# Attention mixing of a spectral attention layer: rounds made ahead, transposes spread, loads moved forward, image products moved to the end

## The chip, the cores and the metric

The kernel runs on one core of one Trainium2 chip. The metric is device time in microseconds of one execution of the whole program, the median over three runs; lower is better.

The core has a tensor engine (PE in the profile; its weight loads are listed as PEld), a vector engine (DVE), a scalar engine (ACT), a general engine (POOL) and an engine that issues most transfers (SP; its queue is SPq). Each runs its own instructions in order, and they meet through semaphores. Transfers between the chip's DRAM and the on-chip memory (SBUF) are carried by 16 DMA engines. Matmuls write to PSUM, a small memory of eight banks, from which DVE and ACT read.

## What is computed

Two layers run one after the other, each added to its input. The first is a state-space layer with a scan and takes most of the time; it is not touched. The second is an attention layer on spectra. Cut to what matters, with B*T = 4*48 images of 48 x 128 and 32 heads:

```python
k = _fno_layer(xa_n, wK, wKs, bKs, (H // 2, W // 2))
q = _fno_layer(xa_n, wQ, wQs, bQs, (H // 2, W // 2))
v = _fno_layer(xa_n, wV, wVs, bVs, (H, W))
qs, ks, vs = (to_seq(q), to_seq(k), to_seq(v))       # B, 32 heads, T, h*w
scores = jnp.einsum('bhtd,bhsd->bhts', qs, ks) / np.sqrt(ks.shape[-1])
attn_w = jax.nn.softmax(scores, axis=-1)
out = jnp.einsum('bhts,bhsd->bhtd', attn_w, vs)
projd = _fno_layer(out, wP, wPs, bPs, (H, W))
attention = _inorm(projd + xa, norm_g[1], norm_b[1])
an = _inorm(attention, norm_g[2], norm_b[2])
m = _fno_layer(an, wM0, ...)                          # two more spectral layers, with norms and a gelu
m = _fno_layer(m, wM1, ...)
output = _inorm(m, norm_g[5], norm_b[5]) + attention
```

`_fno_layer` is a product of low frequencies with complex weights, plus a product of the images with one number per head. Since V, the attention and P are linear in the spectra, the kernel never makes V: it forms for each head the product of the weights of V and P (`dgt`), multiplies the spectra `dxt` by it, and mixes over heads and source images with the attention weights.

## The kernel before

**Queues and planner.** The program is written with tiles; the framework makes the semaphores and the addresses. An instruction emitted through `nc.` is placed by a planner: each engine takes, in the planner's own simulated time, the earliest instruction of the program that is ready there, so a later one may run ahead of one that waits. What is emitted through `on.` keeps the program's order. A tile with a tag has `bufs` buffers; a new one waits until the last reader of the tile that had its buffer is done. Pools lie over each other like a stack: when a pool is closed, the next takes its space, and its tiles wait for the last readers of what lay there.

**Opening (about 3710 to 3886 us).** Images are loaded and normed, their spectra `a2` made, the weight products made (`products`), and for the scores `qs`, `ks` and `s0`. Constants lie in the pools `const` and `small`.

**Scores (L1447 to L1544), pairs of images.** For each of two pairs: twelve steps `jn`. In each, two products `f` of 128 x 1536 (L1490; on POOL for every third `jn`, on DVE otherwise; five buffers) and 16 matmul records into `sc`, four PSUM banks with one buffer (L1497); then eight small products `s0` by `d_qk` of 48 rows (16 records, L1508). Between them the generator `keys` makes `dxt`: for each of 4 images and 4 groups `k`, eight products of `a2` with `fh` (L1462; 48 rows; 256 records in all), ACT copies (L1469), a POOL sum (L1474) and a write to DRAM (L1475); the tile `xt` and its bank have one buffer each. Of its 32 parts 18 are drawn in the first pair and 14 in the second. Then the softmax of the pair, group by group `g`: maximum, difference, exponential (ACT), sum, reciprocal, product `sn`, three transposes `pat` (L1535) and an ACT copy to `attn_c` (L1538). The next pair's `sc` needs the banks that these read.

**Mixing (L1551 to L1660).** 24 steps (k, pair, q), four rounds g each: 96 rounds. `fetch` (L1594) loads the spectra `xrep` of the next step in two transfers of 576 KB, two buffers; `fetch_weights` (L1585) loads `grep`, 576 KB each, six buffers: four at the start, and for a later k two at (k-1, 1, 1) and two at (k-1, 1, 2). These calls are all made at one place, where a step begins, and SP keeps their order. A round:

```python
nc.scalar.copy(gp[:, :, 0:NC], r[:, 0:2])                       # L1624: grep to PSUM
nc.vector.tensor_mul(v, gp[...], x[:, :, 0:2])                  # L1626: 128 x 1536
nc.gpsimd.tensor_mul(v3, r[:, 2:3]..., x[:, :, 2])              # L1630: 128 x 768
nc.tensor.matmul(acc[c][64 * b : ...], attn_c[...], v or v3)    # L1634: c in 0..2, b in 0..1
```

The matmuls of a round are 12 records; `v`, `v3` and `gp` have two buffers. After each twelve rounds (a block: one k, one pair) comes a **turn**: ACT copies `acc[0]` to `s1`, DVE makes three combinations from `s1` and from `acc[1]`, `acc[2]` in PSUM (L1645 to L1647), eight transposes (records `pz`, four and four, L1652) and two ACT copies bring them to `z2`. `acc` has one buffer per c, so the next block's matmuls wait for these readers. At k = 1 each pair has 48 records `pa` of image products (`mix_of_images`, L1564), and ACT copies them to `a0_bd`.

**The rest (from L1667).** Inverse transforms along h (`pe_p`, with the constant `ih`) and along w (`iw2`), then the two further spectral layers. `iw2`, `fw64` and `ih` are loaded at L1675, L1677 and L2094.

Of the kernel before, what the change touches and what calls it, by code (L numbers as in the profile page):

```python
# [962 lines left out]
def layer1(ctx, tc, io, x1_dram, out):  # L963
# [15 lines left out]
    small = ctx.enter_context(tc.tile_pool(name="l1_small", bufs=2, side="right"))  # L979
# [21 lines left out]
    gmat = load("gmat1", [128, 128], io["c_group"])  # L1001
# [5 lines left out]
    mean_m = const.tile([128, 32], F32, name="mean_m")  # L1007
    nc.gpsimd.memset(mean_m, 1.0 / (H * W))
    over_h = const.tile([H, H], F32, name="over_h")
    nc.gpsimd.memset(over_h, 1.0 / H)  # L1010
    over_w = const.tile([128, T], F32, name="over_w")
    nc.gpsimd.memset(over_w, 1.0 / W)

    g_of = const.tile([128, 2, 128], F32, name="g_of")
# [128 lines left out]
    a0_bd = const.tile([96, 2, 96], F32, name="a0_bd")  # L1143
    zp = ctx.enter_context(tc.tile_pool(name="l1_z", bufs=1))
# [18 lines left out]
    dxt = dram.tile([B, 4, T, 3 * NC], F32, name="dxt")  # L1163
# [12 lines left out]
    s0 = pe.tile([T, B, T], F32, name="s0")  # L1176
# [38 lines left out]
    def products():  # L1215
# [5 lines left out]
        with ExitStack() as pw:  # L1221
# [19 lines left out]
            nc.scalar.copy(n_col, pn[:, 0:4].rearrange("p (s z) -> p s z", z=2))  # L1241

# [59 lines left out]
    with ExitStack() as ph:  # L1302
# [133 lines left out]
        for b in range(B):  # L1436
            bs = slice(b * T, (b + 1) * T)
            p = psum.tile([128, 512], F32, tag="mm", name=f"ps0_{b}")
            for j in range(4):
                for c in range(2):  # L1440
                    v = plain[:, j, c, bs]
                    nc.tensor.matmul(p[0:T, 0:T], v, v, start=(j == 0 and c == 0), stop=False)
            nc.tensor.matmul(p[0:T, 0:T], u32[:, bs], u32[:, bs], start=False, stop=True)
            nc.scalar.copy(s0[:, b], p[0:T, 0:T])


    with ExitStack() as ph:  # L1447
        p2 = ph.enter_context(tc.tile_pool(name="l1_p2", bufs=2))
        pf = ph.enter_context(tc.tile_pool(name="l1_pf", bufs=5))
        ps_1 = ph.enter_context(tc.tile_pool(name="l1_ps1", bufs=1, space=PSUM))  # L1450
        pst = ph.enter_context(tc.tile_pool(name="l1_pst", bufs=2, space=PSUM))
        psx = ph.enter_context(tc.tile_pool(name="l1_psx", bufs=1, space=PSUM))

        def keys():

            for b in range(B):
                for k in range(4):
                    xt = p2.tile([T, 3, NC], F32, tag="xt", name=f"xt{b}_{k}", bufs=1)
                    for e in range(2):
                        p = psx.tile([128, 512], F32, tag="xt", name=f"pxt{b}_{k}_{e}")  # L1460
                        for i in range(4):
                            nc.tensor.matmul(  # L1462
                                p[0:T, i * 96 : (i + 1) * 96],
                                a2[:, 8 * k + 4 * e + i, b * T : (b + 1) * T],
                                fh,
                                start=True,
                                stop=True,
                            )
                        nc.scalar.copy(  # L1469
                            xt[:, 0:2].rearrange("t c (k y) -> t k c y", y=48)[:, 4 * e : 4 * e + 4],  # L1470
                            p[0:T, 0:384].rearrange("t (k c y) -> t k c y", c=2, y=48),
                        )
                        yield
                    nc.gpsimd.tensor_add(xt[:, 2], xt[:, 0], xt[:, 1])  # L1474
                    nc.sync.dma_start(dxt[b, k], xt.rearrange("r c n -> r (c n)"))  # L1475

        beside = keys()
        gp = ps_1.tile([128, 3, 4, NH], F32, name="gp_qk")
        nc.scalar.copy(gp, g_qk)
        scale = 2.0 * math.sqrt((H // 2) * (W // 2))  # L1480
        for pair in range(2):
            sc = ps_1.tile([128, 4, 512], F32, tag="sc", name=f"sc{pair}")
            for jn in range(12):
                j, n = divmod(jn, 3)
                shape = [128, NH, T]
                on_pool = jn % 3 == 2
                f = []
                for b in range(2):
                    f.append(pf.tile(shape, F32, tag="f", name=f"f{pair}_{jn}_{b}"))
                    (nc.gpsimd if on_pool else nc.vector).tensor_mul(  # L1490
                        f[b],
                        (g_qk if on_pool else gp)[:, n, j, :, None].to_broadcast(shape),
                        ks[:, j, n, 2 * pair + b, None].to_broadcast(shape),
                    )
                for g in range(4):
                    for b in range(2):
                        nc.tensor.matmul(  # L1497
                            sc[64 * b : 64 * b + 64, g, 0 : 8 * T],
                            qs[:, j, n, 2 * pair + b],
                            f[b][:, 8 * g : 8 * g + 8],  # L1500
                            start=(jn == 0),
                            stop=False,
                        )
                for _ in range(2 - jn % 2 if pair == 0 else 1 + jn % 2):
                    next(beside, None)
            for g in range(4):
                for b in range(2):
                    nc.tensor.matmul(  # L1508
                        sc[64 * b : 64 * b + T, g, 0 : 8 * T],
                        s0[:, 2 * pair + b],  # L1510
                        d_qk[:, 8 * g : 8 * g + 8],
                        start=False,
                        stop=True,
                    )
            for g in range(4):
                t = f"{pair}_{g}"
                v = sc[:, g, 0 : 8 * T].rearrange("p (h s) -> p h s", s=T)
                shape = [128, 8, T]
                mx = p2.tile([128, 8], F32, tag="mx", name=f"mx{t}")
                nc.vector.tensor_reduce(mx, v, AX.X, ALU.max)  # L1520
                s = p2.tile(shape, F32, tag="s", name=f"s{t}")
                nc.vector.tensor_sub(s, v, mx[:, :, None].to_broadcast(shape))
                nc.scalar.activation(s, s, AF.Exp, scale=scale)
                sm = p2.tile([128, 8], F32, tag="sm", name=f"sm{t}")
                nc.vector.tensor_reduce(sm, s, AX.X, ALU.add)
                nc.vector.reciprocal(sm, sm)
                sn = p2.tile([128, 3, 16, 8], F32, tag="sn", name=f"sn{t}")
                nc.vector.tensor_mul(
                    sn.rearrange("t q r h -> t h q r"),
                    s.rearrange("t h (q r) -> t h q r", r=16),  # L1530
                    sm[:, :, None, None].to_broadcast([128, 8, 3, 16]),
                )
                p = pst.tile([128, 512], F32, tag="tr", name=f"pat{t}")
                for q in range(3):
                    nc.tensor.transpose(  # L1535
                        p[:, q * 128 : (q + 1) * 128], sn[:, q].rearrange("t r h -> t (r h)"), ident
                    )
# [3 lines left out]
                )  # L1541
        for _ in beside:
            pass
    early.close()  # L1544

# [669 lines left out]
```

## Time and profile before

The three runs took 4520.93, 4521.48 and 4522.82 us; the median is 4521.48.

| | us |
|---|---|
| median of three runs | 4521.48 |
| the profiled execution, its own time | 4536.64 |
| its span, first to last instruction | 4534.9 |
| scores: first f to last copy to `attn_c` | 3886.5 to 4006.8 |
| mixing: first to last `acc` record | 4019.4 to 4262.8 |
| first record of `pe_p` | 4269.8 |
| DMA issues of `xrep`: 48 of 576 KB | 4006.3 to 4247 |
| DMA issues of `grep`: 16 of 576 KB | 4007.6 to 4198 |

How to read it: times of the stages count from the first instruction of the profiled execution. A row of a timeline gives the start, the length, the engine, the line, the operation with the tile that it writes and those that it reads, how many instructions are merged in it, and in brackets how long the engine was idle before it and what ended that. A row of the windows gives a stretch, its length, each engine's busy time with its count of instructions, the clock granted to the tensor engine as a share of full speed, the busy share of the DMA engines and their GB/s. One fp32 matmul or transpose of the program appears as two records.

### The profile page before, as it was taken

To read this page: it belongs to the slowest core of one execution; us is meant where nothing else is said; L and a number is where in the kernel's file an instruction comes from. 1 tells how busy PE (TensorE), PEld (TensorE's weight loads), DVE (VectorE), ACT (ScalarE), POOL (GpSimd) and SP (SyncE) were. 2 spreads that over 40 slices of the span, in tenths; PEclk is the share of its full clock that TensorE was granted. 3 is DMA by queue.
4 is the path that set the end of the run, shared out by engine and by line. 5 is a ranking of instruction groups with operands and counts; after the bars stand their busy time and mean duration, and the time that the engine had idled before them with its cause. 6 is when DMAs were issued, how large, how long until landed. Compare 5 with 4: busy or idle time off the path is not lost.

```text
span 4534.9 us, 73722 instructions
## 1 busy us (share of the span) xinstructions
PE 3854.2 (85%) x26212; PEld 2993.0 (66%) x26212; DVE 3854.3 (85%) x2646; ACT 3439.2 (76%) x6964; POOL 3356.7 (74%) x3523
## 2 busy tenths in 40 slices
PE   6989987888899878888998788878877885979877
PEld 3777776777777767776777677767776762535444
DVE  3888999999899999998999999989999974657446
ACT  3888888988888889887888899879998862323344
POOL 2777788988787889887878898978888961356432
PEclk9989999999999899998999999999999997989877
DMA  2333333333333333333333333434333332155536
GB/s 63 93 94 103 91 100 100 111 96 110 97 106 94 96 102 111 98 110 94 107 93 96 103 107 100 115 94 111 104 105 105 100 111 62 25 128 138 133 101 160
DMA packets 327068, 461.05 MB, mean 102 GB/s; under 512 B 112788, under 2 KB 295636, under 8 KB 325996
## 3 DMA queue, kind: packets, MB, share of 16 engines
q1 hardware_dynamic: 311904, 433.20, 35.0%
q10 hardware_dynamic: 14796, 23.13, 1.5%
q8 instruction: 208, 3.41, 0.3%
q14 instruction: 160, 1.31, 0.1%
HBM read 400.99 MB, written 55.44 MB: 101 GB/s over the span
## 4 chain that ended last, share of the span: by engine, by line
PE 35%; ACT 22%; DVE 21%; issue 12%; POOL 5%; DMA 3%; SPq 1%; ACTq 0%; DVEq 0%; POOLq 0%
DVE h L55 13%; PE yp L55 8%; ACT scaled L55 6%; PE pc L55 5%; DVE db L55 4%; ACT da L55 4%; PE da L55 4%; ACT decay L55 4%; PE pd L55 2%; POOL hc L55 2%; PE acc L1634 2%; ACT dt L55 2%; ACT turned L55 2%; PE pg L55 2%; PE pb L55 2%
## 5 line engine op out<-in xcount | busy, mean ns | idle before, releaser
L55 POOL TENSOR_TENSOR hc<-h,cbc 128x960 f32<-128x960 f32 (+1 forms) x1280 | 2546.1, 1991 | 565.4 <-PE yp L55 194.1
L55 DVE TENSOR_TENSOR_SCAN h<-da,carry,db 128x962 f32<-128x962 f32 (+1 forms) x640 | 1355.9, 2119 | 115.7 <-ACT da L55 97.3
L55 DVE TENSOR_TENSOR_SCAN h<-decay,carry,da 128x962 f32<-128x962 f32 (+1 forms) x640 | 1362.5, 2129 | 6.5 <-PE da L55 6.2
L55 PE MATMUL yp<-ident,hc 128*128 128x128 f32 (+1 forms) x9728 | 1268.6, 283 | 52.9 <-POOL hc L55 49.3
L55 PEld LDWEIGHTS yp<-ident,hc 128*128 128x128 f32 (+1 forms) x9728 | 1140.6, 145 | 217.5 <-issue 109.3
L55 ACT ACTIVATE scaled<-turned,bt 128x256 f32<-128x256 f32 (+1 forms) x2432 | 1035.5, 497 | 27.5 <-ACT turned L55 23.6
L55 ACT ACTIVATE da<-dt,a_neg 128x480 f32<-128x480 f32 (+1 forms) x1280 | 826.1, 645 | 187.9 <-DVE h L55 165.0
L55 ACT ACTIVATE decay<-dt,a_neg 128x480 f32<-128x480 f32 (+1 forms) x1280 | 799.1, 674 | 28.2 <-DVE h L55 23.6
L55 PE MATMUL da<-ident,scaled 128*128 128x128 f32 (+1 forms) x4864 | 646.5, 276 | 194.1 <-DVE h L55 178.5
L55 DVE TENSOR_TENSOR db<-du,pb 128x960 f32<-128x960 f32 (+1 forms) x640 | 699.0, 1092 | 110.1 <-PE pb L55 100.1
L55 PEld LDWEIGHTS da<-ident,scaled 128*128 128x128 f32 (+1 forms) x4864 | 543.8, 145 | 243.0 <-ACT scaled L55 97.9
L55 PE MATMUL pb<-ident,bt 128*128 128x128 f32 (+1 forms) x2432 | 376.6, 276 | 38.4 <-DVE db L55 38.4
L55 PEld LDWEIGHTS pb<-ident,bt 128*128 128x128 f32 (+1 forms) x2432 | 292.7, 141 | 171.4 <-issue 98.2
L55 PE MATMUL pc<-pad,w_c 128*128 128x480 f32 (+1 forms) x720 | 335.9, 581 | 6.5 <-ACT th L55 3.0
L55 POOL TENSOR_TENSOR du<-dt,xc 128x480 f32<-128x480 f32 (+1 forms) x160 | 206.4, 1290 | 49.5 <-ACT dt L55 49.5
L1630 POOL TENSOR_TENSOR v<-grep,xrep 128x768 f32<-128x768 f32 x96 | 174.8, 1823 | 89.8 <-PE acc L1634 47.5
L1634 PE MATMUL acc<-v,attn_c 128*64 128x384 f32 x1152 | 211.1, 502 | 29.4 <-DVE v L1626 15.3
L1626 DVE TENSOR_TENSOR v<-gp,xrep 128x1536 f32<-128x1536 f32 x96 | 167.7, 1756 | 76.4 <-PE acc L1634 43.9
L55 PEld LDWEIGHTS da<-carry,ident 128*128 128x128 f32 x1280 | 201.6, 199 | 0.0
L55 PE MATMUL da<-carry,ident 128*128 128x2 f32 x1280 | 197.6, 224 | 0.0
L55 POOL COPY carry<-h 128x2 f32<-128x2 f32 x1024 | 194.9, 190 | 0.0
L1634 PEld LDWEIGHTS acc<-v,attn_c 128*64 128x64 f32 x1152 | 113.2, 139 | 116.8 <-issue 63.6
(382 smaller groups left out, 3995.9 us busy)
## 6 DMA issues: line engine op xcount, KB each, us to landing
cbc<-cd SPq DMA_DIRECT2D x512, 240.0 KB
cbc<-other SPq DMA_DIRECT2D x512, 240.0 KB
xrep<-dxt SPq DMA_DIRECT2D x48, 576.0 KB
cbc<-cd SPq DMA_DIRECT2D x128, 192.0 KB
cbc<-other SPq DMA_DIRECT2D x128, 192.0 KB
yt<-turned ACTq DMA_DIRECT2D x40, 384.0 KB
old<-yt SPq DMA_DIRECT2D x40, 384.0 KB
grep<-dgt SPq DMA_DIRECT2D x16, 576.0 KB
```

The lines of the kernel that those rows point to most:

```text
L55: return lambda *args, **kw: self._tc.keep_in_program_order(emit(*args, **kw))
L1626: nc.vector.tensor_mul(v, gp[:, None, :, 0:NC].to_broadcast([128, 2, 2, NC]), x[:, :, 0:2])
L1630: nc.gpsimd.tensor_mul(v3, r[:, 2:3].to_broadcast([128, 2, NC]), x[:, :, 2])
L1634: nc.tensor.matmul(acc[c][64 * b : 64 * b + 64, 0:NC], attn_c[:, 2 * pair + b, g, q], v[:, b, c] if c < 2 else v3[:, b], start=first, stop ...
```

## The change

- **keys** makes `dxt` for two images at once: 96 rows instead of 48, hence 64 products instead of 128, 16 ACT copies, 8 sums, 8 writes; `xt` and its bank get two buffers. All 16 parts are drawn in the first pair. `dxt` is laid out by pairs.
- **Scores**: the products with `s0` come first, with `s0` padded to 64 columns, and no longer last.
- **Softmax in two halves**: `open_soft` (maximum, difference, exponential, for all four g) right after a pair's scores; `close_soft` (sum, reciprocal, product, transposes, copy) of the first pair inside the second pair's loop after jn = 1, 3, 5, 7, that of the second pair at the start of mixing.
- **Spectra of two steps ahead**: `ahead`, in the buffer that `a2` had, is loaded with the `xrep` of steps 0 and 1 at jn = 1 of the second pair. Later steps are fetched as before when the step before begins; `grep` of the next k is fetched one at a time, at four places. The fetches are emitted through `nc.sync`.
- **Mixing one round ahead**: `make(n + 1)` (fetches, `gp`, `v`, `v3`) is emitted before `use(n)` (the matmuls). At a turn ACT copies all three `acc` to SBUF; DVE's combinations come one round later, the first four transposes two rounds later, the second four after two more.
- **Image products last**: `mixing` makes both pairs' products after the last round, two images at once, 48 records; a mask `own` keeps the blocks (DVE, twice). `e_w` is made twelve rounds before the end. `own` costs two products and a copy in `products`.
- **Constants**: `iw2`, `fw64`, `ih` are loaded in the opening. Several opening constants move to `small`, whose pool is closed after the opening; the softmax's pool takes that side.

```diff
@@ keys
-            for b in range(B):
+                for pair in range(2):
                 for k in range(4):
-                    xt = p2.tile([T, 3, NC], F32, tag="xt", name=f"xt{b}_{k}", bufs=1)
+                        xt = p2.tile([96, 3, NC], F32, tag="xt", name=f"xt{pair}_{k}")
...
-                                a2[:, 8 * k + 4 * e + i, b * T : (b + 1) * T],
+                                    a2[:, 8 * k + 4 * e + i, pair * 96 : (pair + 1) * 96],
@@ scores
+                for g in range(4):
+                    for b in range(2):
+                        nc.tensor.matmul(
+                            sc[64 * b : 64 * b + 64, g, 0 : 8 * T],
+                            s0[:, 2 * pair + b],
+                            d_qk[:, 8 * g : 8 * g + 8],
+                            start=True,
...
-                for _ in range(2 - jn % 2 if pair == 0 else 1 + jn % 2):
-                    next(beside, None)
+                    if pair and jn == 0:
+                        ahead = zp.tile([128, 2, 2, 3, NC], F32, tag="z96", name="ahead")
+                    for _ in range(2 * (pair == 0 and jn % 3 != 2)):
+                        next(beside, None)
+                    if pair and jn == 1:
+                        for i in range(2):
+                            fetch(i, ahead[:, i])
+                    if pair and jn % 2 and jn < 8:
+                        close_soft(0, jn // 2)
+                for _ in beside:
+                    pass
+                open_soft(pair, sc)
@@ mixing
+            def make(n):
+                i, g = rounds[n]
+                k, pair, q = steps[i]
+                if g == 0 and i != 2 and i + 1 < len(steps):
+                    fetch_x(i + 1 + (i < 2))
+                if k < 3 and g == 0 and (pair, q) in ((0, 1), (0, 2)):
+                    fetch_weights(k + 1, q - 1)
+                r, x = gs[k, g], xs[i]
+                gp = ps_g.tile([128, 2, 512], F32, tag="gp", name=f"gp{t}")
+                nc.scalar.copy(gp[:, :, 0:NC], r[:, 0:2])
+                v = p2.tile([128, 2, 2, NC], F32, tag="v", name=f"v{t}")
+                nc.vector.tensor_mul(v, gp[:, None, :, 0:NC].to_broadcast([128, 2, 2, NC]), x[:, :, 0:2])
+                v3 = p2.tile([128, 2, NC], F32, tag="v3", name=f"v3{t}")
+                nc.gpsimd.tensor_mul(v3, r[:, 2:3].to_broadcast([128, 2, NC]), x[:, :, 2])
+                made[n] = v, v3
+                if k < 3 and (pair, q) == (1, 2) and g < 2:
+                    fetch_weights(k + 1, 2 + g)
+            def use(n):
...
+                s = planes(f"s{pair}_{k}")
+                for c in range(3):
+                    nc.scalar.copy(s[:, c], acc[c][:, 0:NC])
+                def combine():
+                    a1, a2, a3 = (s[:, c].rearrange("p (k y) -> p k y", y=48) for c in range(3))
+                    nc.vector.tensor_sub(zt[:, :, 0], a1, a2)
+                    nc.vector.tensor_add(a1, a1, a2)
+                    nc.vector.tensor_sub(zt[:, :, 1], a3, a1)
...
+                after.extend((combine, lambda: turn_over(0), None, lambda: turn_over(1)))
+            for g in range(4):
+                fetch_weights(0, g)
+            for g in range(2):
+                close_soft(1, g)
+            make(0)
+            for n in range(len(rounds)):
+                if n < 2:
+                    close_soft(1, 2 + n)
+                if n + 1 < len(rounds):
+                    make(n + 1)
+                todo = after.popleft() if after else None
+                use(n)
+                if todo:
+                    todo()
+                if n == len(rounds) - 12:
+                    e = weights_of_mixing()
+            mixing(e)
+            for todo in after:
+                if todo:
+                    todo()
@@ constants, in the opening
+    for i in range(2):
+        nc.scalar.dma_start(iw2[64 * i : 64 * i + 64], io["c_IW"])
+    ih = const.tile([96, 96], F32, name="ih")
+    nc.sync.dma_start(ih, io["c_IH"])
```

## The prediction

> **What bounds the kernel now.** I read first the busy time by windows, cut at the stages that the change touches.
>
> ```profile
> 3886.50:3937.00 50.50, 46.69 (x328) 26.68 (x328) 34.26 (x20) 8.32 (x16) 32.54 (x17) 1.00 0.14 32
> 3937.00:3945.00 8.00, 4.56 (x25) 3.03 (x26) 7.49 (x17) 3.15 (x7) 0.99 (x1) 0.71 0.24 55
> 3945.00:3994.00 49.00, 46.09 (x317) 25.49 (x314) 22.88 (x16) 7.95 (x18) 25.08 (x13) 0.98 0.12 28
> 3994.00:4007.00 13.00, 4.52 (x17) 2.12 (x13) 10.06 (x24) 3.87 (x9) 2.58 (x5) 0.67 0.07 17
> 4007.00:4019.40 12.40, 0.01 (x2) 0.02 (x2) 1.18 (x1) 0.80 (x1) 1.81 (x1) 0.50 0.97 225
> 4019.40:4263.00 243.60, 227.30 (x1304) 127.68 (x1304) 176.92 (x118) 87.26 (x119) 172.98 (x95) 0.95 0.62 144
> ```
>
> Columns: PE, PEld, DVE, ACT, POOL, clock, DMA share, GB/s. PE bounds both score loops and the mixing. Between them lie two softmax stretches in which DVE works, and 12.4 us in which only transfers run; the granted clock falls to 0.50 there. Next, the timeline at that hand-over and at a turn:
>
> ```profile
> 4006.31 0.48 ACT L1538 COPY attn_c<-pat 128x384 f32<-128x384 f32 x1 [1.34 <-PE pat L1535]
> 4006.35 1.23 SPq L55 DMA_DIRECT2D xrep<-dxt  x2
> 4007.63 3.04 SPq L55 DMA_DIRECT2D grep<-dgt  x4
> 4017.39 0.80 ACT L1624 COPY gp<-grep 128x768 f32<-128x768 f32 x1 [10.60 <-DMA grep<-dgt]
> ...
> 4049.64 1.50 PE L1634 MATMUL acc<-v,attn_c 128*64 128x384 f32 x4 [1.10 <-DVE v L1626]
> 4051.08 0.65 PE L1652 MATMUL pz<-ident,zt 128*96 128x128 f32 x4
> 4051.65 0.87 PE L1634 MATMUL acc<-v,attn_c 128*64 128x384 f32 x4
> 4052.45 0.64 PE L1652 MATMUL pz<-ident,zt 128*96 128x128 f32 x4
> ```
>
> The first mixing transfers are issued only when the last softmax copy starts: their buffers lie over the softmax's. At a turn PE stalls, then alternates between transposes and the next block. Last, DVE:
>
> ```profile
> 4076.92 1.76 DVE L1626 TENSOR_TENSOR v<-gp,xrep 128x1536 f32<-128x1536 f32 x1 [3.79 <-DMA xrep<-dxt]
> ...
> 4089.76 1.76 DVE L1626 TENSOR_TENSOR v<-gp,xrep 128x1536 f32<-128x1536 f32 x1 [0.17 <-PE acc L1634]
> 4091.71 1.76 DVE L1626 TENSOR_TENSOR v<-gp,xrep 128x1536 f32<-128x1536 f32 x1 [0.19 <-PE acc L1634]
> 4093.64 1.76 DVE L1626 TENSOR_TENSOR v<-gp,xrep 128x1536 f32<-128x1536 f32 x1 [0.18 <-PE acc L1634]
> ```
>
> A steady round takes 1.935 us (start to start) and DVE waits for PE: 12 records of 0.161. Taking every twelfth `acc` start from PE's timeline, the mixing's 243.6 us are 96 x 1.935 = 185.8 and 57.8 more: first four rounds 4.9; seven turns 30.1 (each 9.1/7 = 1.3 of `pz` and 2.06 of stall, and 6.5 in all at the three that follow a transfer wait, at clock 0.50); four rounds that wait for `xrep`, 9.1; two rounds with `pa`, 9.4; the rest 4.3.
>
> **The change part by part.**
>
> *Scores, first pair.* The pair runs from the first full `f` (3889.9) to its last score record (3932.0) and then shares 5.2 us with `s0` until the softmax starts at 3937.3. `s0` (16 records, 2.6 us) moves under the wait for the first `f`: free; without that cover, 2.6. All `keys` now fall here: 128 records, of which 16 run in the opening as before. Eight now take 0.86 us. With 96 weight columns instead of 48 the nearest row is `pi_p` (128 columns, moving 96), 0.135 per record, against 0.107 now; I take 0.12, bounds 0.107 and 0.135. So 112 x 0.12 = 13.4 (12.0 to 15.1) plus 192 x 0.161 = 30.9, plus 0.5 of stall: last score at 3934.7, 2.6 before the present softmax start. ACT's present 44.8 us of waiting for `dxt` writes goes with the second buffer, off PE's path.
>
> The Trainium skill, "TensorE: Matmul & The Clock Gate", section "LDWEIGHTS (loading the stationary operand)", speaks against the wider `keys`: a weight load grows with its columns (columns / 1.2 ns), which would add an estimated 40 ns to each of the 112 records, to 0.147, and 3 us to the sum. The weight loads here only partly agree: `pxt` with 48 columns shows 123 ns, `pe_p` with 96 columns 163, `pz` with 96 columns 127.
>
> *Between the pairs.* Now 3937.3 to 3944.5, when the second pair's records begin. `open_soft` holds the banks for four times maximum and difference, 1.07 apart: 4.3 us, to 3939.2. Then `s0` is on the path: 2.6, or 5.1 at the half clock that followed the present 2.5 us pause; I take 5.1. Score records begin at 3944.3: the 2.4 won come back here.
>
> *Second pair.* Now 3944.5 to 3994.97. It loses 14 parts of `keys` (14 x 0.86 = 12.0) and `s0` (its 16 records, broken by `keys` at 0.6 a time: 4.3), and keeps 30.9 and four `pat` groups, 4 x 0.7. End: 3944.3 + 33.7 = 3978, **17 earlier**. DVE must make 12 `f` by jn 7 and four `close_soft` of 1.6: 27.5 us less about 4.4 made ahead, against PE's 5 + 7 x 2.6: even. If DVE leads, it costs up to 6; if the turnover is warm, 2.5 more is won. The four early `xrep` transfers (2.36 MB, 10 us at 235 GB/s) queue on SP behind eight `dxt` writes that are over by then.
>
> *Hand-over.* From the last score record to the first `acc`: now 4019.4 - 3995.0 = 24.4. After: `open_soft` 4.4, two `close_soft` 3.3, `v` 1.8, semaphores 0.2: 9.7. `grep` lies over `f` and not over the softmax, so it starts with the last score record. Now two `xrep` and a `grep` (1.77 MB, 7.5 us at 235 GB/s) are used 11.0 us after the first issue, so 3.5 go to issue and latency; one `grep` alone needs 3.5 + 2.5, then `gp` 0.8: `v` could start at 6.8, DVE is free at 7.7 and is last. **14.7 earlier**. If `grep` waits for the softmax after all, 8 to 9 of it are lost.
>
> *Mixing.* The first three rounds share DVE with two `close_soft`: 3.4 each instead of 1.935, +4.4, and half clock +1.6: 6. A turn: ACT copies release `acc[0]` 0.25 + 0.48 + 0.15 after the last record, and the matmuls run c by c behind the copies: 0.9, I take 1.0. DVE's three combinations (1.75 with gaps) come while v(n + 1) is ready; were they put ahead of it, each turn would cost that much more, 12 in all. `gp` queues behind ACT's three copies only if the planner puts it there (0.8 more). `pz` stays 9.1. Transfers: a step needs 7.5 us from issue (4090.36) to use (4097.9), and four rounds last 7.74: hidden. A lone `grep` makes it 7.5 us of bytes in a step that, turns included, lasts 8.4; only (k, 1, 2) carries two, 10 us: I take 2 in all, 0 to 30. With no transfer wait the half clock at turns goes: 0. `pa` leaves: 0 here. Sum: 185.8 + 9.1 + 6 + 7 + 2 + 4.3 = 214.2 against 243.6: **29.4 less**.
>
> The Trainium skill, "DMA: Bandwidth & Descriptors", section "Specifications", allows some 358 GB/s from DRAM per core, by which a pair of `xrep` would be an estimated 3.3 us and transfers would never show. The row contradicts it: 225 GB/s at a share of 0.97, and 235 in the fullest stretches. I keep 5.0 us a pair.
>
> *End.* From the last `acc` to the first `pe_p`: now 6.9, closed by `ih`, issued at 4267.3. After: copies 1.7, combinations 2, then two times transposes and copy 2.3 each, with `mixing` under them on PE (48 records at 0.12 to 0.135, 6): 8. +1.1. But PE no longer idles, and the first eight `pe_p` records ran at half clock, 0.64 instead of 0.32: -2.5. `iw2` was not waited for (`pi_p` waits for `e_p` at 4288): 0. **-1.4**, bounds -4 to +2.
>
> *Opening.* `own` and its copy sit among PE's transposes, memsets on an idle POOL, two `iw2` issues hold ACT for 1.26: **+1**, 0 to 2.
>
> Sum: -17 - 14.7 - 29.4 - 1.4 + 1 = -61.5. The profiled execution took 4536.6 (span 4534.9 plus 1.7) and becomes 4475.1. It stood 15.2 above the median of the runs; keeping that, **4460**.
>
> **The rivals.**
>
> *Transfers become the mixing's bound.* For: with two `grep` ahead of it and two behind, `xrep` took from 4065.56 to 4076.9, 11.4 us; four rounds last 7.74, and a faster mixing asks for 35 MB in 214 us where it had 38 in 256. Against: steps without `grep` hide all but 0.2 to 0.7. Price: each of the 12 later `grep` shows its own 2.5 us: +30, 4490.
>
> *It does not do what it says*: the planner already ran a round ahead. For: `v` of round 12 starts at 4045.42, before the first combination at 4047.37. Then turns keep 2.06 (+7.4) and only the loads, `keys` and `pa` pay: 4467; with `grep` still waiting for the softmax, 4476.
>
> *Slower: prefetch broken by SP's order.* The fetches are no longer kept in order. If a `grep` that waits for its buffer stands in SP's queue ahead of the next `xrep`, that one is issued only when it is needed: 7.5 us bare in each of 22 steps, 165 in all. It decides from 61.5 / 22 = 2.8 us per step. At half of it, 3.75 x 22 = 82: 4542. Against: a `grep` is emitted only where a buffer is free or its last reader has just been emitted.
>
> **How the numbers follow.** Forecast 4460, own range 4444 to 4478: chance 0.58. Planner already ahead, 4467 to 4476: 0.14. Transfers, 4478 to 4505: 0.17. Slower by SP's order: 0.08. No change within 0.2% (9 us; less a measurement of this kernel cannot tell): 0.03. Faster: 0.58 + 0.14 + 0.17 = 0.89. The range for 8 in 10 goes from 4435 (warm turnover, end at -4, turns at 0.9, narrower `keys` at 0.107, no transfer wait, some clock gain in the rest) to 4492.
>
> **What would show it.** Right: first `acc` some 10 us after the last score record; rounds of 1.935 with turns of about 4.2; no `xrep` release above 1 us on DVE; `pe_p` some 63 us earlier; the rest from there still 265. Wrong: SP issuing `xrep` late, `grep` issued after `attn_c`, DVE's combinations ahead of `v`, or second-pair scores waiting on DVE `f`.

## The result and the profile after

The changed kernel takes 4479.88 us, the median of four runs (4467.85 to 4482.42), against 4522.15 for the kernel before beside it (4520.93 to 4529.98): ratio 0.9898, interval 0.9877 to 0.9919. Five more runs gave 0.9897 (0.988 to 0.9914). It is faster by 1.0%, 42 to 46 us; 4460 was predicted, within 4435 to 4492 (own range of the forecast: 4444 to 4478).

The profiled execution of the changed kernel took 4479.64 us. Its busy time by windows, in the columns used before (PE, PEld, DVE, ACT, POOL, clock, DMA share, GB/s):

```profile
3881.60:3929.40 47.80, 47.80 (x337) 25.71 (x336) 32.74 (x19) 9.07 (x18) 29.83 (x16) 1.00 0.24 71
3929.40:3931.50 2.10, 0.47 (x4) 0.00 (x0) 1.53 (x1) 0.00 (x0) 1.45 (x1) 1.00 1.04 255
3931.50:3936.60 5.10, 0.17 (x2) 0.20 (x4) 5.00 (x12) 1.85 (x4) 1.31 (x1) 0.67 1.02 264
3936.60:3946.50 9.90, 9.90 (x32) 3.63 (x33) 3.06 (x8) 0.24 (x1) 0.00 (x0) 0.50 0.30 68
3946.50:3978.90 32.40, 32.40 (x190) 13.81 (x188) 23.57 (x14) 1.91 (x4) 19.77 (x7) 0.99 0.00 1
3978.90:3986.50 7.60, 1.37 (x6) 0.54 (x4) 6.88 (x16) 3.10 (x6) 1.81 (x1) 0.86 0.79 184
3986.50:4206.20 219.70, 211.71 (x1217) 89.45 (x1217) 185.83 (x126) 93.91 (x136) 175.29 (x95) 0.99 0.65 156
```

Rows one and five are the score loops. Rows two to four are the pause between the pairs and what follows it: 7 us almost without PE, then 9.9 us in which PE is always busy and the clock is 0.50. Row six is the hand-over, row seven the mixing. The pause on the timeline:

```profile
3929.97 1.76 DVE L1572 TENSOR_TENSOR f<-gp_qk,ks 128x1536 f32<-128x1536 f32 x1 [0.91 <-PE sc L1579]
...
3931.64 0.55 DVE L1482 TENSOR_REDUCE mx<-sc 128x8 f32<-128x384 f32 x1
...
3936.43 4.11 PE L1558 MATMUL sc<-d_qk,s 48*64 48x384 f32 x12 [6.56 <-DVE sm L1493]
```

DVE makes an `f` of the next pair before it reads the first bank, and PE stands still for 6.56 us. The hand-over:

```profile
3979.40 0.56 DVE L1482 TENSOR_REDUCE mx<-sc 128x8 f32<-128x384 f32 x1 [6.65 <-PE sc L1579]
3979.43 2.44 SPq L1645 DMA_DIRECT2D grep<-dgt  x4
...
3984.60 1.81 POOL L1669 TENSOR_TENSOR v<-grep,ahead 128x768 f32<-128x768 f32 x1 [8.08 <-DVE sn L1495]
...
3986.46 1.54 PE L1685 MATMUL acc<-v,attn_c 128*64 128x384 f32 x2 [0.95 <-POOL v L1669]
```

`grep` is issued 0.6 us after the start of the last score record (before: 13.1), and the first `acc` follows that record by 7.6 us where it was 24.9. Its release is the product of GpSimd (POOL in the rows); the records that need DVE's `v` start at 3988.77. A turn of the mixing, on DVE:

```profile
4071.59 1.75 DVE L1667 TENSOR_TENSOR v<-gp,xrep 128x1536 f32<-128x1536 f32 x1
4073.26 0.73 DVE L1701 TENSOR_TENSOR zt<-s 128x384 f32<-128x384 f32 x1
4073.91 1.74 DVE L1667 TENSOR_TENSOR v<-gp,xrep 128x1536 f32<-128x1536 f32 x1
4075.57 1.31 DVE L1702 TENSOR_TENSOR s<-s 128x384 f32<-128x384 f32 x1
4076.81 1.75 DVE L1667 TENSOR_TENSOR v<-gp,xrep 128x1536 f32<-128x1536 f32 x1
4078.48 0.54 DVE L1703 TENSOR_TENSOR zt<-s 128x384 f32<-128x384 f32 x1
4078.95 1.75 DVE L1667 TENSOR_TENSOR v<-gp,xrep 128x1536 f32<-128x1536 f32 x1
4081.58 1.76 DVE L1667 TENSOR_TENSOR v<-gp,xrep 128x1536 f32<-128x1536 f32 x1 [0.89 <-ACT gp L1665]
```

There is no idle time in brackets from the first combination to 4080.7: DVE sets the pace here. In a steady round it idles 0.16 to 0.2 us; three combinations bring 2.58. On PE, the same turn:

```profile
4072.97 5.38 PE L1685 MATMUL acc<-v,attn_c 128*64 128x384 f32 x32 [0.29 <-ACT s L1696]
4078.61 0.86 PE L1685 MATMUL acc<-v,attn_c 128*64 128x384 f32 x2 [0.26 <-DVE v L1667]
4079.40 0.64 PE L1709 MATMUL pz<-ident,zt 128*96 128x128 f32 x4
```

The four rounds of this turn take 2.49, 1.94, 2.36 and 4.01 us, 10.80 together: 3.06 above four steady ones, of which some 1.3 are `pz`. The old turn took 5.30, 1.99 and 2.26 in three rounds, 3.75 above.

The stages of the two profiled executions side by side:

| us | before | after | change | predicted |
|---|---|---|---|---|
| layer 0, to its last scan | 3707.1 | 3699.7 | -7.4 | 0 |
| opening, to the first `f` | 179.4 | 181.9 | +2.5 | +1 |
| scores, first `f` to last `sc` | 108.0 | 97.3 | -10.8 | -17 |
| hand-over, last `sc` to first `acc` | 24.9 | 7.6 | -17.3 | -14.7 |
| mixing, first to last `acc` | 243.4 | 219.6 | -23.8 | -29.4 |
| last `acc` to first `pe_p` | 7.1 | 8.0 | +1.0 | +1.1 |
| first `pe_p` to the end | 265.0 | 263.7 | -1.3 | -2.5 |

Without layer 0, which the change doesn't touch, 49.7 us are gone of the 61.5 in the sum.

### The profile page after: what moved, and what is told of

Its sections match the earlier page's. It is cut to its first block, busy times and chain, and to the rows that moved or that the text cites. A ratio compares the mean times of both kernels' runs of the same rounds, so it can differ in the third digit from the quotient of the medians.

```text
span 4477.8 us, 73316 instructions
## 1 busy us (share of the span) xinstructions
PE 3826.1 (85%) x26040; PEld 2941.2 (66%) x26040; DVE 3858.7 (86%) x2648; ACT 3436.4 (77%) x6963; POOL 3350.4 (75%) x3515
## 5 line engine op out<-in xcount | busy, mean ns | idle before, releaser
L55 PE MATMUL pb<-ident,bt 128*128 128x128 f32 (+1 forms) x2432 | 377.2, 277 | 37.2 <-DVE db L55 37.1
L1669 POOL TENSOR_TENSOR v<-grep,xrep 128x768 f32<-128x768 f32 x88 | 162.6, 1852 | 35.3 <-PE acc L1685 24.3
L55 PE MATMUL pd<-xd,w_dt 40*128 40x480 f32 (+1 forms) x320 | 172.0, 618 | 16.3 <-ACT bt L55 7.4
L1667 DVE TENSOR_TENSOR v<-gp,xrep 128x1536 f32<-128x1536 f32 x88 | 153.6, 1754 | 27.6 <-PE acc L1685 11.1
```

The costliest lines, as they stand in the source:

```text
L55: return lambda *args, **kw: self._tc.keep_in_program_order(emit(*args, **kw))
L1667: nc.vector.tensor_mul(v, gp[:, None, :, 0:NC].to_broadcast([128, 2, 2, NC]), x[:, :, 0:2])
L1669: nc.gpsimd.tensor_mul(v3, r[:, 2:3].to_broadcast([128, 2, NC]), x[:, :, 2])
```

## The experiments

One profile of each kernel gives the stages; they repeat within 1.8 us between two profiles of one kernel, while whole runs of one kernel differ by 9 to 36. "Scores" is first `f` to last `sc`, "rest" last `sc` to last `acc` (hand-over and mixing together, since some edits shift time between the two). Ratios are to the kernel before.

| run | scores | rest | median, ratio with interval |
|---|---|---|---|
| before / e1_before_again | 108.0 / 108.2 | 268.3 / 266.7 | 4522 to 4533 |
| after / e1_after_again | 97.3 / 96.4 | 227.2 / 226.2 | 4479.81, 0.9897 (0.988 to 0.9914) |
| e1_turn_old | 96.4 | 233.3 | 4482.33, 0.9906 (0.989 to 0.9923) |
| e1_spread | 97.3 | 234.0 | 4484.12, 0.9902 (0.9884 to 0.992) |
| e2_ordered | 97.3 | 227.5 | 4487.90, 0.9906 (0.9875 to 0.9937) |
| e2_psum_mid | 97.3 | 226.2 | 4474.92, 0.9887 (0.985 to 0.9924) |
| e2_keys_pause | 97.7 | 226.3 | 4482.78, 0.9902 (0.9871 to 0.9933) |
| e2_mix_best | 97.2 | 215.4 | 4472.96, 0.9884 (0.9846 to 0.9923) |
| e3_sc_banks | 89.1 | 226.4 | 4474.98, 0.9871 (0.9843 to 0.9898) |
| e3_no_ahead | 96.6 | 231.5 | 4486.84, 0.9894 (0.987 to 0.9917) |
| e3_best | 89.1 | 213.0 | 4457.96, 0.9824 (0.98 to 0.9848) |
| e4_order_spread | 97.1 | 219.4 | 4467.11, 0.9869 (0.9842 to 0.9896) |

The intervals of whole runs overlap for most of these; what is said of an edit rests on its stage in one profile.

**The two kernels again.** No edit.

> The kernel before, unchanged, looked at a second time. Theory A (the 15 us between its profiled execution and the median of its plain runs came from that one execution): the profiled span is within 5 us of 4521 this time, and the first product of the scores' opening comes some 7 us earlier than in the first profile. Theory B (the profiler adds about 15 us to this kernel every time): the profiled execution is again 4534 to 4539.

4508.26 us, 28.4 below the first profiled execution; 25.7 of it lie ahead of the first `f` (3860.7 against 3886.5). Theory A holds in kind, though not in its number (within 5 us of 4521): the offset belonged to the one execution, not to the profiler. Over all fourteen profiles the first `f` comes at 3860.7 to 3891.7, with a layer 0 that is the same in all. What varies in layer 0 wasn't tried.

> The changed kernel, unchanged, in five rounds beside the kernel before. Both theories expect a ratio of 0.988 to 0.991; if the single run of 4467.85 among the four shown was no stray, the runs fall into two groups some 12 us apart and a profile of the faster group has a mixing stage or an opening that is shorter by that amount.

4472.45 to 4481.97. There are no two groups; 4467.85 belongs to the same spread.

**The turn as before.**

```diff
-for c in range(3):
-    nc.scalar.copy(s[:, c], acc[c][:, 0:NC])
+nc.scalar.copy(s[:, 0], acc[0][:, 0:NC])      # the combinations read acc[1], acc[2]
-after.extend((combine, lambda: turn_over(0), None, lambda: turn_over(1)))
+combine(); turn_over(0); turn_over(1)
```

> Only the turn-over between two blocks of the mixing is put back: one copy by ScalarE, the three combinations straight from PSUM, the transposes in the round that follows at once. Everything else stays changed. Theory A (the late turn is worth what the rounds at the turns shrank by, some 5.3 + 1.98 + 2.26 - (2.49 + 1.94 + 2.36 + 4.01 - 1.94) = 0.7 us each after what it gives back, over 7 turns): 3 to 8 us slower than the changed kernel. Theory B (the late turn is the main part of the mixing's 23.8 us): 12 to 20 us slower. Theory C (the late turn gives back all that it saves, because its combinations read both operands from SBUF and take up to 1.3 us, and stand between the products on VectorE): within 2 us of the changed kernel. The records of the three combinations take 0.54 to 0.56 us each here by all three.

The rest takes 233.3, 6.1 to 7.1 more: theory A. The rounds at a turn take 5.3, 1.99 and 2.26 us again, as in the kernel before, so the late turn does what the planner's running ahead had not done. It is worth about a quarter of the mixing's gain. DVE at a turn of this run:

```profile
4064.73 0.56 DVE L1700 TENSOR_TENSOR zt<-s,acc 128x384 f32<-128x384 f32 x1
4065.20 1.75 DVE L1667 TENSOR_TENSOR v<-gp,xrep 128x1536 f32<-128x1536 f32 x1
4066.87 0.54 DVE L1701 TENSOR_TENSOR s<-s,acc 128x384 f32<-128x384 f32 x1
4067.52 0.56 DVE L1702 TENSOR_TENSOR zt<-acc,s 128x384 f32<-128x384 f32 x1
4069.98 1.76 DVE L1667 TENSOR_TENSOR v<-gp,xrep 128x1536 f32<-128x1536 f32 x1 [1.91 <-PE acc L1685]
```

Here DVE has time to wait for PE (1.91), and the combinations, with an operand in PSUM, take 0.54 to 0.56.

**The combinations one at a time.**

```diff
-after.extend((combine, lambda: turn_over(0), None, lambda: turn_over(1)))
+after.extend((combine[0], None, combine[1], None, combine[2], None,
+              lambda: turn_over(0), None, lambda: turn_over(1)))
```

> The three combinations of a turn-over are no longer issued together but one in every second round, and the two transposes two rounds after one another behind them. Theory A (the turns cost 1.9 us each because up to three combinations of 0.5 to 1.3 us stand in one round ahead of the products on VectorE): each turn shrinks to 1.0 us or less, 5 to 8 us faster than the changed kernel. Theory B (the turns cost what they cost by the ScalarE copies and the transposes on TensorE): within 2 us. Theory C (the sum over the turn is bound by the amount of VectorE work): within 2 us, with the same idle time of TensorE spread over more rounds.

The blocks after the first, third and fifth turn took 26.46, 25.60 and 26.51 us against 26.72 to 26.79, 26.39 to 26.55 and 27.43 to 27.54, some 0.3 to 1.0 shorter. But the blocks at 4040 and 4100 took 34.6 and 32.2. SP's queue ahead of the first of them:

```profile
4028.32 1.16 SPq L1517 DMA_DIRECT2D xrep<-dxt  x2
4030.25 7.77 SPq L1645 DMA_DIRECT2D grep<-dgt  x4
4038.13 10.63 SPq L1517 DMA_DIRECT2D xrep<-dxt  x4
```

The planner put four `grep` together ahead of the next `xrep`, and DVE then waited 6.08 us for `xrep`; four more at 4091.29 cost another 4.64. (In the changed kernel three `grep` stand together ahead of an `xrep` at 4035.04 and 4090.65, and its two longest waits for `xrep`, 2.77 and 2.44 us, come next.) No theory foresaw that; the total says nothing on the three until the order is mended.

**The written order, and an operand in PSUM.**

```diff
# e2_ordered: fetch_x and fetch_weights
-nc.sync.dma_start(...)
+on.sync.dma_start(...)
# e2_psum_mid: the second accumulator goes to the bank of the transposes
+sm = pst.tile([128, 512], F32, tag="tr", ...)
-nc.scalar.copy(s[:, 1], acc[1][:, 0:NC])
+nc.scalar.copy(sm[:, 0:NC], acc[1][:, 0:NC])
-nc.vector.tensor_add(a1, a1, a2); nc.vector.tensor_sub(zt[:, :, 1], a3, a1)
+nc.vector.tensor_add(a2, a1, a2); nc.vector.tensor_sub(zt[:, :, 1], a3, a2)   # a2 is sm
```

> The mixing's fetches are kept in the order in which they are written, as before the change; all else is the changed kernel, whose mixing (first to last acc record) took 219.6 and 218.8 us in two profiles. Theory A (the planner's hoisting of grep ahead of the next xrep costs the waits for xrep): the four waits of VectorE for xrep of over 1 us go, the mixing shrinks by 3 to 6 us. Theory B (the bytes in flight are the limit, not their order): the waits stay, within 1 us. Theory C (the free order was a gain of its own, since an ordered grep that waits for its buffer holds back the xrep behind it): 2 us or more longer.

The mixing itself is 4.0 to 4.8 shorter (214.9), as A said, but 3.6 to 3.9 of that lie in its first block (26.2 against 29.8 to 30.1), and the hand-over is 12.6 instead of 7.4 to 7.6: the last copy to `attn_c` now comes with the first `acc`, where it came 13 us behind it. The rest is 227.5, unchanged. The order alone is worth nothing: B in effect, as the waits for `xrep` went from 6.9 us to 4.7 only.

> At a turn the second accumulator is copied into the PSUM bank that the transposes use afterwards instead of into SBUF, so that each of the three combinations has one operand in PSUM; nothing else differs from the changed kernel. Theory A (two SBUF operands beside a working GpSimd are what makes the combinations take 0.54 to 1.31 us): all 24 records take 0.54 to 0.56, VectorE wins some 0.9 us at each turn and the mixing shrinks by 4 to 7 us. Theory B (they are long because of something else that happens at a turn, ScalarE's copies for one): the records stay up to 1.3 us long and the mixing stays within 1 us.

All 24 combinations take 0.54 to 0.56 us (0.54 to 1.32 in the changed kernel), so the two operands in SBUF are what made them long; GpSimd's part is in the last section. A turn shrinks from 10.80 to 10.1 (2.28, 1.93, 2.97, 2.92). But the mixing keeps 218.5: the blocks with a transfer to wait for gave it back (28.2 and 28.0 at the second and fourth turn, as in the changed kernel; 27.3 at the sixth, against 25.9 to 26.5).

**The three edits together, and without the PSUM operand.**

> Three edits of the mixing at once: fetches in their written order, one operand of each combination in PSUM, and the combinations one in every second round with the transposes after them. If the order alone made the spread combinations lose at the second and fourth turn (7.8 and 6.4 us in one round), and VectorE's extra work is what a turn costs (2.5 us of combinations against 0.2 us of slack in a round), the mixing takes 205 to 212 us against 219 now. If the turn's cost is TensorE's transposes and ScalarE's copies, 215 to 219. If spreading delays the release of what the next transfer needs, 220 or more.

> Written order of the fetches and the combinations one in every second round, with both operands of each combination in SBUF as in the changed kernel: the run with the three edits of the mixing, less the PSUM operand. There the stretch from the last sc to the last acc record took 215.4 us, in the changed kernel 227.2 and 226.2, with the spread combinations alone 234.0. Theory A (order and spreading together do it, and the longer combinations fit into ten rounds' slack of 0.2 us each): 215 to 217.5. Theory B (the PSUM operand is what makes the combinations fit): 219 to 224. Theory C (the order alone mended nothing in the spread kernel): 230 or more.

With all three the mixing takes 203.3, a little less than the 205 to 212 expected, and the rest 215.4, 10.9 to 11.9 less than the changed kernel. The second and the fourth block take 24.8 us (26.4 to 26.8 in the changed kernel), where twelve steady rounds and `pz` are 24.5: little is left there of the combinations. With both operands in SBUF again it is 219.4. So, against 226.2 to 227.2: order 0, PSUM operand 0 to -1, spreading +7 to +8, order and spreading -7 to -8, all three -11 to -12. The edits don't add. A likely reason: a round ends when the last of PE, DVE and the transfer is done, and what is taken from one alone is waited for at another. Theory B of the last run (219 to 224) is met at its edge: the operand is worth 4.0 once the rest is out of its way.

**The pause between the pairs.**

```diff
# e2_keys_pause
-for _ in range(2 * (pair == 0 and jn % 3 != 2)): next(beside, None)
+for _ in range(pair == 0 and jn % 2): next(beside, None)
# and in open_soft, after each of the four g
+for _ in range(3): next(beside, None)
# e3_sc_banks
-sc = ps_1.tile([128, 4, 512], F32, tag="sc", ...)
+sc = [ps_1.tile([128, 512], F32, tag=f"sc{g}", ...) for g in range(4)]
```

> Ten of the sixteen parts of the keys' transform are moved from between the first pair's products into the pause after them, while VectorE takes maxima and differences; nothing else differs from the changed kernel, where the scores (first to last sc record) took 97.3 and 96.5 us, the opening products of the second pair 5.4 and the rest of that pair 37.1. Theory A (the 6 us that the scores' stage won less than the sum said are TensorE's half clock after an idle pause): the granted clock stays at 1.0 through the pause, the 16 opening products of the second pair take 2.6 to 3.0 and the rest 33 to 34.5, and the first pair loses some 10 x 0.4 = 4 us of products; 8 to 11 us less in all. Theory B (the second pair is bound by VectorE, which makes the f and closes the softmax): it stays at 42 to 43 us whatever the clock, only the first pair shrinks, by 4.

The first pair's products end 8.4 us sooner, but from the second pair's first record to its last it takes 49.9 instead of 41.6 to 42.5, and the scores stay at 97.7. Both theories fall. The windows:

```profile
3933.30:3935.70 2.40, 0.03 (x1) 0.03 (x1) 2.33 (x6) 1.39 (x4) 2.28 (x2) 1.00 0.33 108
3935.70:3937.90 2.20, 2.20 (x18) 1.67 (x18) 2.20 (x5) 1.13 (x3) 0.99 (x1) 0.96 0.64 189
3937.90:3954.40 16.50, 15.62 (x61) 8.30 (x62) 2.43 (x7) 3.17 (x7) 2.97 (x3) 0.50 0.51 147
3954.40:3987.20 32.80, 32.80 (x193) 14.15 (x190) 23.57 (x14) 1.92 (x4) 19.77 (x7) 0.99 0.20 54
```

PE was idle for 2.39 us and later once more for 0.88 (ACT's copies of the keys waited for the writes of `xt`). Some 2 us after it was busy again the clock fell to 0.50 for some 17 us. Filling the pause in part did not keep the clock up, and the half clock was longer than in the changed kernel. Of the 7.4 to 8.3 us more in the second pair, 5.6 are two parts of the keys that came between the opening products at half clock, and 0.88 the second pause.

> The scores of a pair are four tiles of one PSUM bank instead of one tile of four, so that the maximum and the difference of a bank can start when that bank's products are over, and the next pair's opening products when that bank is read; nothing else differs from the changed kernel (pause between the pairs' products 6.6 us, opening products 5.4, rest of the second pair 37.1, from last sc to first acc record 7.4 to 7.6). Theory A (the second pair pays for TensorE's half clock, and the half clock for a pause of over 2 us): pause 3 to 4.5 us and still the half clock, since 2.4 us were enough in the run with the keys in the pause; scores 3 to 5 us shorter, hand-over 1 us shorter. Theory B (what counts is TensorE's busy share over some us, and products in between hold the clock): clock 1.0 throughout, opening products in step with VectorE, rest of the pair 33 to 34.5: scores 8 to 11 us shorter. Theory C (VectorE's order is what holds the pause, since an f and a sum stand in it): within 1 us.

```profile
3875.00:3922.60 47.60, 47.60 (x336) 26.34 (x336) 32.97 (x20) 9.06 (x18) 29.83 (x16) 1.00 0.24 71
3922.60:3930.00 7.40, 6.67 (x38) 2.42 (x36) 6.95 (x14) 1.97 (x4) 3.06 (x2) 1.00 1.03 280
3930.00:3964.10 34.10, 32.68 (x188) 14.55 (x184) 27.84 (x22) 2.10 (x5) 19.09 (x7) 1.00 0.06 16
```

PE's pause is 0.73 us, the clock is 1.00 in every window, and the scores take 89.1: 7.3 to 8.1 less, at the lower edge of theory B. From the second pair's first record to its last it is 40.3 instead of 41.6 to 42.5: most of the gain is the pause itself (6.56 to 0.73), for at full clock DVE has become the limit in places (PE 32.68 busy of 34.10). The hand-over is unchanged, 7.4.

**Without the loads ahead.**

```diff
-ahead = zp.tile([128, 2, 2, 3, NC], F32, tag="z96", name="ahead")
-for i in range(2): fetch(i, ahead[:, i])
# mixing
+fetch_x(0)                                   # before the first grep
-if g == 0 and i != 2 and i + 1 < len(steps): fetch_x(i + 1 + (i < 2))
+if g == 0 and i + 1 < len(steps): fetch_x(i + 1)
```

> The spectra of the first two steps are no longer loaded during the second pair's products; the first is fetched ahead of the weights when the mixing's buffers are free, the second one step ahead like all others. Nothing else differs from the changed kernel (last sc to first acc 7.4 to 7.6 us, first block of the mixing 29.8 to 30.1). Theory A (the hand-over is bound by the softmax's work on VectorE, transfers of 5 us a pair fit under it): within 2 us of the changed kernel over hand-over and first block. Theory B (the loads ahead are what closes the hand-over): two xrep and a grep take 11 us from issue to use as before the change, so the first acc comes 4 to 6 us later and the second step waits again for its own: 5 to 9 us in all.

The first `acc` comes 13.3 us after the last `sc`, 5.7 to 5.9 later, and the rest is 4.3 to 5.3 longer: theory B at or just below its lower edge. Its second half did not come: the first block takes 29.1 us, no longer than in the changed kernel. The loads ahead are worth about 5 us, all of it at the hand-over.

**All edits.** The three edits of the mixing and the score banks.

> The three edits of the mixing (written order of the fetches, one PSUM operand in each combination, combinations spread) and the scores in four tiles together. From last sc record to last acc record 227.2 us in the changed kernel and 215.4 with the three edits; with the four tiles some 1 less. If the edits add up: scores 92 to 94 instead of 97, from last sc to last acc 213 to 216, end unchanged: 14 to 18 us below the changed kernel, ratio to the kernel before 0.986 or a little lower. If the time won in the scores comes back as another wait at the hand-over: 10 to 13 below.

They add up, to a little more than the 14 to 18 expected: scores 89.1, rest 213.0, together some 21 us below the changed kernel. 4457.96 us, ratio 0.9824 (0.98 to 0.9848); this interval lies below those of the changed kernel. DVE at a turn of this run:

```profile
4042.83 0.55 DVE L1702 TENSOR_TENSOR zt<-s,sm 128x384 f32<-128x384 f32 x1 [0.31 <-ACT sm L1697]
4043.76 1.76 DVE L1667 TENSOR_TENSOR v<-gp,xrep 128x1536 f32<-128x1536 f32 x1 [0.38 <-PE acc L1685]
4045.44 0.55 DVE L1703 TENSOR_TENSOR sm<-s,sm 128x384 f32<-128x384 f32 x1
4045.90 1.75 DVE L1667 TENSOR_TENSOR v<-gp,xrep 128x1536 f32<-128x1536 f32 x1
4048.45 1.76 DVE L1667 TENSOR_TENSOR v<-gp,xrep 128x1536 f32<-128x1536 f32 x1 [0.81 <-DMA xrep<-dxt]
4050.13 0.54 DVE L1704 TENSOR_TENSOR zt<-s,sm 128x384 f32<-128x384 f32 x1
```

Between the combinations DVE now waits for others; the waits for `xrep` are 0.8 us at most.

## Why the prediction was nearly right

The direction, the stages and their order of size held, and the time fell in the range; the forecast was 20 us too low. About 12 are terms of the sum, about 8 the offset between the profiled execution and the median (15.2, less the 7.4 by which layer 0 was shorter). The time lies 2 us above the forecast's own range, in the stretch given to the rival of the transfers, but most of what is missing is not the transfers'.

- **First pair.** Right in its end: its last record starts 47.8 us after the first `f` and ends at 48.3; the working had it end at 48.2. That is in part luck, since errors cancel. The products began 1.2 us sooner than the working had it and the `keys` took 12.3 us instead of 13.4, while the 192 products took 0.17 us each with the changes between them, not 0.161, 1.8 us more. The `keys` records took 0.096 us each (16 in 1.53), below the 0.107 to 0.135 of the bounds, and all 128 ran in the pair, not 112. The estimate of 0.147 from the Trainium skill's rule on weight loads ("TensorE: Matmul & The Clock Gate", "LDWEIGHTS (loading the stationary operand)") went the wrong way: the loads grew from 123 to 165 ns, by about the 40 of the rule, but the distance between records did not grow with them.
- **Between the pairs and second pair.** Mis-sized: -10.8 instead of -17. The pause was taken at 4.5 and was 6.6, since the planner puts an `f` of 1.76 us ahead of the first maximum and a sum of 0.54 ahead of the last difference. The half clock was taken for the opening products alone, 5.1 us (they took 5.4), but it lasted until 10.4 us after PE had started again, into the products after them, which took 37.1 instead of 33.7. PE is busy in all of that stretch, so the 5.1 us at half speed behind the opening products are 2.6 of those 3.4. Some 0.4 more are the four groups of transposes, 0.8 each instead of 0.7; the small remainder wasn't pinned down. The run with separate banks has neither the pause nor the half clock, and is 7.3 to 8.1 us shorter.
- **Hand-over.** Right in its mechanism, and in its size too: the 9.7 were reckoned to DVE's `v`, whose first records start 9.9 us after the last `sc`; the 7.6 to the first `acc` record of all rest on GpSimd's product. In the kernel before the first `acc` record rested on GpSimd's product too, so the gain, taken alike, is 17.3 and not the 14.7 of the sum. That `grep` no longer waits for the softmax is shown by its issue at 3979.43; that the loads ahead matter is shown by the run without them.
- **Mixing.** -23.8 instead of -29.4. The failed step is "DVE's three combinations (1.75 with gaps) come while v(n + 1) is ready". They do, but they then stand ahead of v(n + 2), and DVE has some 0.2 us of slack per round. They also take 2.58 instead of 1.75 in the turn shown, because both operands now come from SBUF. Counted by the starts of the rounds, the five turns without a longer wait for `xrep` take 1.2 to 1.8 us beyond four steady rounds and `pz`, the two with one (at 4043 and 4098) 3.4 and 3.0: 14.3 in all, where the sum had 7 for the turns and 2 for transfers. That is nearly all of the 5.4 us by which the mixing is longer than the 214.2 of the sum. Some 3 of the 14.3 are the transfers' part in those two turns, against the 2 taken; the larger part is DVE's. The first rounds (6.9 instead of 6) and the "rest" (3.7 instead of 4.3) nearly cancel. The rival that said that turns keep 2.06 was nearer than the sum's 1.0, though for another reason.
- **End and opening.** +1.0 and -1.3 against +1.1 and -2.5; +2.5 against +1.
- **The offset.** "It stood 15.2 above the median of the runs; keeping that" was a wrong step: the second profile of the kernel before lay 14 below the median, and the changed kernel's own profile lay on it. Layer 0 was 7.4 us longer in the first profile than in that of the changed kernel.
- **Rivals.** Transfers didn't become the bound (6.9 us of waits, not 30). SP's order didn't break the prefetch here, but the run with the spread combinations shows that rival alive: two `xrep`, each behind four `grep`, cost 6.1 and 4.6 us.
- **Its signs.** Of those for being right, the turns (a round with what a turn adds: 4.5 to 5.0 us for 4.2, and 6.2 to 6.6 in the two that wait longer), the waits for `xrep` (2.77, 2.44 and 1.05, where none above 1 was to come) and `pe_p` (55.7 us earlier, not 63) failed. Of those for being wrong, the combinations ahead of `v` came.

## What to carry to other kernels

When work is moved off a stalled engine's path, count the slack per round of the engine that takes it: three small instructions of 0.5 to 1.3 us in successive rounds are not hidden by 0.2 us each, but short ones, one in every second round and with the transfers in time, nearly are. Where a round has several limits close together, edits that do nothing alone, or harm, can be worth 11 us together, so try them in combination. One tile over several PSUM banks makes the next user wait for all of them; a tile per bank closed a pause of 6.6 us to 0.73, and the half clock behind it went too.

## What the hardware showed that was not expected

- **Clock.** A pause of PE of 6.56 us was followed by 10.4 us at a granted clock of 0.50 in which PE was always busy (8.7 in the second profile). After a pause of 2.39 us the clock fell to 0.50 only when PE had been busy again for 2 us, and stayed there for some 17 us, with PE idle for 0.88 of them. With 0.73 us of pause the clock stayed at 1.00. The Trainium skill ("TensorE: Matmul & The Clock Gate", "What's actually happening") has half speed after about 3.4 us of idle time and full speed after about 3.4 us of work. Here a shorter pause was followed by half speed too, and both half clocks outlasted that much work; the measurement decides. Why they last so long stays open.
- **VectorE beside GpSimd.** A combination of 128 x 384 with both operands in SBUF took 0.54 to 1.32 us in the changed kernel, with one in PSUM always 0.54 to 0.56. The traces show what decides. Eight profiles have both operands in SBUF. In them 92 combinations started with more than 0.16 us of a GpSimd product still to run, and each ended 0.41 to 0.42 us after that product. All others took 0.54 to 0.56, those behind the last round among them, where GpSimd is idle:

```profile
4128.85 1.84 POOL L1669 TENSOR_TENSOR v<-grep,xrep 128x768 f32<-128x768 f32 x1 [0.74 <-PE acc L1685]
4130.11 0.99 DVE L1702 TENSOR_TENSOR s<-s 128x384 f32<-128x384 f32 x1
...
4206.50 0.56 DVE L1701 TENSOR_TENSOR zt<-s 128x384 f32<-128x384 f32 x1 [2.55 <-ACT s L1696]
```

With an operand in PSUM 0.54 to 0.56 held even with 1.8 us of a product to run. GpSimd pays as well: its products with `xrep` took up to 2.18 us in the changed kernel, and 1.81 to 1.84 in the four kernels with an operand in PSUM. The Trainium skill ("SBUF — State Buffer", "SBUF: two separate sides") says that a VectorE instruction with two SBUF inputs and a GpSimd instruction that reads SBUF exclude each other on a shared port, and that the one that starts first holds it to its end. The records agree.
